# Attention and experts on one core: the experts inside the branch's arms, and the second half's rows in places of their own, read a block ahead

## The chip, the core and the metric

The kernel runs on one core of a Trainium2 chip. Five engines work side by side, each on its own stream of instructions: TensorE (PE) multiplies matrices into PSUM and takes weights in a parallel stream (PEld), VectorE (DVE) and ScalarE (ACT) work elementwise and read PSUM, GpSimd (POOL) makes masks, small sums and the indirect gathers, and SyncE (SP) issues most DMAs. Engines wait for each other by semaphores. The metric is device time in microseconds (us) of one execution; lower is better.

## The reference, cut to what matters

```python
x = L0_attn_x                                     # 2048 tokens x 512
x = layernorm(x + attention(x))                   # 16 heads of 32, causal, q and k of unit norm, rope on every second head
x = layernorm(x + experts(x))

def experts(x):
    scores = softmax(x @ gate_w)                  # 8 experts
    w, e = top_k(scores, 2)
    routed = sum over the two of  w * ((silu(x @ w_gate[e]) * (x @ w_up[e])) @ w_down[e])    # hidden 352
    shared = (silu(x @ sw_gate) * (x @ sw_up)) @ sw_down                                      # hidden 704
    return routed + shared
```

All of it is float32, and layernorm has no weights.

## The kernel before

**A branch, and what follows it.** The kernel loads x and the weights, looks whether all gains of q are small enough for a softmax with a bound fixed in advance, and reads that comparison (`choice`, L1510) into a register of every engine. `tc.If(bounded > 0)` (L1514) then runs `fast_attention`; the other arm (`general_attention`) is not run with these inputs, but lies in the program. Behind the join, `sparse_moe` is called once for both arms (L1537).

**Attention.** `fast_attention` is one long list of steps whose order on PE is written out by hand: x is transposed (L112), multiplied to q, k and v (L126, the rows `fps_qkv`), normed and rotated, and then scores (L331), exponentials (ACT, L341) and values (L376) run in units of heads and 512 keys. At its end come the output product, the first layer norm, the transposes of the result (x1T) and the gate logits (L286). The result goes to DRAM in rows (`x1d`) and, for the second half, transposed (`x1Td`). Into PE's free places of that end the kernel puts six "fillers" (`first_block`, L1452): the six up products of the shared expert's block 0. The shared expert's weights are loaded (`load_shared_expert`, L633) by `x_is_read`, as soon as the space of the transposed x is free.

**The shared expert.** It works in eight blocks b of two tiles (256 tokens). `shared_up_piece` (L664 to L685) makes one of six pieces j of a block's hidden values: a gate product and an up product (8 matmul instructions each, in the rows `ps_gs` and `ps_us`), silu on ACT (L675), the product of the two on DVE (L677; L683 to L685 for the narrow sixth). The PSUM pool for it, `ps_gu`, has two buffers of each kind, so PE's product j + 2 waits until DVE has multiplied piece j. `shared_down` (L964 to L982) multiplies a block's hidden values by the down weights, into one PSUM bank per tile, and hands each to a function `done`.

**First half, routing, experts.** `sparse_moe` (L708) begins with tables (L733 to L766), then makes the softmax of the logits (L796 to L803) and the two largest (L813 to L817) on DVE and ACT, counts the tokens of each expert and gives each a place (L842 to L906). Beside it PE runs blocks 1 to 3 of the shared expert and the down products of blocks 0 to 3. What they give is added to x1 and put away in DRAM (`accd`). Then 36 tiles of 128 routed tokens follow (`routed`, L1116): rows are gathered from `x1d` (L1005), transposed, multiplied by the weights of the tile's expert, whose place PE reads from a table, and written to `yd`. If the routing needs more tiles, a second branch (L1159) runs them; with these inputs it does not.

**Second half.** L1166 to L1185 run blocks 4 to 7 of the shared expert, and with them the end of all 16 tiles: a tile's sum takes two gathered rows of `yd` per token, weighted (`with_experts`, L1041), then the layer norm (L776, of which `inv_sqrt`, L594, is eleven DVE operations on 128x1) and the write to `out` (L1053). In block b the first piece is followed by the last block's down product, by the reads of the block's rows of x1 and of the old sums of the first half (`read_rows`, L1055), and by the read of the next block's x1T (`read_block`). Each later piece is followed by one of four items: two `early_rows` (the gathered rows are added to x1 of this block's tiles) and two `old_rows` (they are added to an old sum, which is then normed and written). Rows and old sums take turns in a pool of five buffers, gathered rows in a pool of four.

**What sets the order.** Where the text says `tc.manual_schedule`, the named engines run the instructions in the order of the program text; the others get an order from a planner. In `sparse_moe` PE and SP are fixed by hand, and DVE, ACT and POOL are planned. Within an engine the order never changes at run time.

## Time and profile before

Three executions took 1158.70, 1160.28 and 1161.79 us: the median is 1160.28. The profile is of another execution.

| quantity | before |
|---|---|
| profiled execution | 1160.72 us |
| its span | 1159.0 us |
| PE busy | 1114.8 us, 96% |
| DVE, ACT, POOL busy | 603.9, 502.3 and 193.0 us |
| mean granted clock of PE | 0.992 of full speed |
| PE's first instruction of the first tile | 5.86 us |
| attention's last product (logits) / first product behind the join | 631.12 / 634.93 us |
| first product of the second half in PE's main flow (block 4, L664) | 1031.19 us |
| last down product's end / last write issued | about 1149.7 / 1155.10 us |

The profile's lines read as follows. A line of the timeline gives the start, the duration, the engine, the line of the program, the operation, the tiles (result<-operands) and their shape; xN means that N equal instructions stand together. In brackets stands how long the engine had been idle before, and what released it: "<-DVE big L677" is DVE's instruction of line 677, "<-issue" means that the profile shows nothing that it waited for. Queues have a q behind their engine's name. The clock column, PEclk, is the share of full speed that the chip granted PE; in a window in which it is 0.50 a matmul takes twice as long.

### The profile page before, as it was taken

The numbers are of one execution on the slowest core, as the hardware profiler recorded it, in microseconds if no ns is written. First come the engines' busy times: TensorE is split into PE (matmuls) and PEld (weight loads), VectorE is DVE, ScalarE is ACT, GpSimd is POOL, SyncE is SP. The second block draws the span as 40 slices with busy tenths as digits, with TensorE's granted clock in tenths as the row PEclk, the third lists the DMA queues.
The fourth block names the chain that finished last, engine by engine and source line by source line (L and its number), as shares of the span: only waits on it lengthen the run. The fifth ranks groups of instructions, "written<-read, shape, count | busy, mean of one in ns | idle before, by whom it ended". The sixth has DMA issues, their size and how long they took to land.

```text
span 1159.0 us, 15359 instructions
## 1 busy us (share of the span) xinstructions
PE 1114.8 (96%) x5692; PEld 584.8 (50%) x5692; DVE 603.9 (52%) x948; ACT 502.3 (43%) x847; POOL 193.0 (17%) x207
## 2 busy tenths in 40 slices
PE   7999999999999999999998999999999999999996
PEld 4543333333343333333355777556656565666664
DVE  1566796777777786797856341111111111115666
ACT  3576777878778777665642100111112111110000
POOL 0321213210321213101020010101011010022331
PEclk9998999999999999999999999999999999999999
DMA  9000000000000110122113595322221221033553
GB/s 302 17 1 1 1 1 1 1 1 1 1 1 1 46 46 10 66 64 73 55 47 130 190 329 174 116 64 72 64 64 64 64 67 61 28 121 100 154 162 127
DMA packets 50227, 83.71 MB, mean 72 GB/s; under 512 B 8032, under 2 KB 22368, under 8 KB 50144
## 3 DMA queue, kind: packets, MB, share of 16 engines
q1 hardware_dynamic: 43904, 64.39, 16.3%
q0 software_dynamic: 5440, 17.83, 5.3%
q8 instruction: 50, 0.82, 0.3%
q10 hardware_dynamic: 800, 0.39, 0.2%
q14 instruction: 33, 0.27, 0.1%
HBM read 59.79 MB, written 22.81 MB: 71 GB/s over the span
## 4 chain that ended last, share of the span: by engine, by line
PE 77%; DVE 8%; issue 7%; ACT 3%; DMA 2%; POOL 2%; SPq 0%; POOLq 0%; DVEq 0%; ACTq 0%
PE fps_qkv L126 12%; PE fps_s L331 9%; PE ps_dr L1031 8%; PE ps_gr L1129 7%; PE ps_ur L1129 7%; PE fps_av L376 7%; PE ps_ds L972 6%; PE ps_us L664 5%; PE ps_gs L664 4%; PE fps_o L229 4%; DVE facc L367 3%; ACT big L341 2%; PE ps_xT L1014 1%; DMA y<-yd,slot_i 1%; PE fps_qkT L204 1%
## 5 line engine op out<-in xcount | busy, mean ns | idle before, releaser
L341 ACT ACTIVATE big<-fps_s,neg_gmax 128x1024 f32<-128x1024 f32 (+3 forms) x320 | 296.7, 983 | 85.8 <-PE fps_s L331 84.4
L367 DVE TENSOR_TENSOR facc<-facc,big 128x2048 f32<-128x2048 f32 (+3 forms) x128 | 250.1, 1954 | 58.3 <-POOL big L352 28.9
L126 PE MATMUL fps_qkv<-big,shared 128*128 128x384 f32 x512 | 183.7, 502 | 1.6 <-ACT facc L403 0.8
L331 PE MATMUL fps_s<-big 32*128 32x512 f32 (+3 forms) x1280 | 174.3, 581 | 0.7 <-ACT big L211 0.7
L376 PE MATMUL fps_av<-big 128*32 128x512 f32 (+3 forms) x1280 | 138.2, 538 | 13.8 <-POOL big L352 11.7
L126 PEld LDWEIGHTS fps_qkv<-big,shared 128*128 128x128 f32 x512 | 93.1, 192 | 85.7 <-issue 17.3
L1016 DVE COPY xT<-ps_xT 128x512 f32<-128x512 f32 x34 | 23.5, 691 | 171.3 <-PE ps_xT L1014 171.3
L352 POOL TENSOR_SCALAR_AFFINE_SELECT big<-big 128x512 f32<-128x512 f32 x64 | 61.7, 965 | 306.1 <-ACT big L341 305.7
L331 PEld LDWEIGHTS fps_s<-big 32*128 32x128 f32 x1280 | 55.7, 184 | 92.8 <-issue 53.6
L1031 PE MATMUL ps_dr<-big,hT 128*128 (+1 forms) x216 | 98.7, 593 | 0.5 <-ACT hT L1024 0.5
L1039 ACT COPY y<-ps_dr 128x512 f32<-128x512 f32 x36 | 21.1, 585 | 166.3 <-PE ps_dr L1031 166.3
L1129 PE MATMUL ps_gr<-big,xT 128*128 x288 | 91.2, 459 | 0.0
L1129 PE MATMUL ps_ur<-big,xT 128*128 x288 | 91.2, 459 | 0.0
L376 PEld LDWEIGHTS fps_av<-big 128*32 128x32 f32 x1280 | 31.5, 109 | 106.2 <-issue 76.8
L675 ACT ACTIVATE acts<-ps_gs 128x256 f32<-128x256 f32 x35 | 13.4, 383 | 155.0 <-PE ps_gs L664 150.8
L664 PE MATMUL ps_us<-big,shared 128*128 128x256 f32 x336 | 78.6, 380 | 1.5 <-DVE big L677 1.5
L1005 POOL DMA_INDIRECT rows<-x1d,rows_of x36 | 34.2, 950 | 260.0 <-PE ps_xT L1014 211.9
L1129 PEld LDWEIGHTS ps_gr<-big,xT 128*128 128x128 f32 x288 | 54.4, 189 | 40.4 <-issue 17.1
L664 PE MATMUL ps_gs<-big,shared 128*128 128x256 f32 x280 | 68.7, 389 | 3.5 <-DVE big L760 3.5
L664 PEld LDWEIGHTS ps_us<-big,shared 128*128 128x128 f32 x336 | 63.7, 190 | 10.9 <-DVE big L677 2.3
L1129 PEld LDWEIGHTS ps_ur<-big,xT 128*128 128x128 f32 x288 | 51.9, 190 | 22.8
L1031 PEld LDWEIGHTS ps_dr<-big,hT 128*128 128x128 f32 (+1 forms) x216 | 41.0, 190 | 42.6 <-issue 34.4
(188 smaller groups left out, 1112.6 us busy)
## 6 DMA issues: line engine op xcount, KB each, us to landing
yd<-y SPq DMA_DIRECT2D x36, 256.0 KB, 2.0
big<-in_L_ffn_w_gate_dram SPq DMA_DIRECT2D x8, 704.0 KB, 10.4
big<-in_L_ffn_w_up_dram SPq DMA_DIRECT2D x8, 704.0 KB, 10.4
big<-in_L_attn_x_dram SPq DMA_DIRECT2D x16, 256.0 KB, 4.4
fres<-in_L_attn_x_dram SPq DMA_DIRECT2D x16, 256.0 KB, 2.8
x1d<-big SPq DMA_DIRECT2D x16, 256.0 KB, 2.0
big<-in_L_ffn_w_down_dram SPq DMA_DIRECT2D x8, 512.0 KB, 7.5
x<-x1d SPq DMA_DIRECT2D x12, 256.0 KB, 2.9
```

The costliest lines, as they stand in the source:

```text
L126: nc.tensor.matmul(ps[0], xT[:, t, c * P : (c + 1) * P], wq_sb[c].rearrange("p (s m) -> p s m", s=3)[:, :, g * P : (g + 1) * P], start=(c ...
L229: nc.tensor.matmul(ps[0], xs[t][:, g * P : (g + 1) * P], wo_sb[:, g, :], start=(g == 0), stop=(g == NC - 1))
L331: nc.tensor.matmul(pss[n][i // 2][:, i % 2, off:], k_at[(g * NB + kb) % KV][r, kl, :], q_at[u % Q][r, off:], start=True, stop=True,)
L341: nc.scalar.activation(pr_at[n % PR][:, 2 * j : 2 * j + 2, off:], pss[n][j][:, :, off:], AF.Exp, bias=neg_gmax)
L352: nc.gpsimd.affine_select(d, d, [[0, 4], [1, P]], ALU.is_ge, 0.0, base=0, channel_multiplier=-1)
L367: nc.vector.tensor_tensor(acc[:, :, off:], first[:, :, off:], pr[:, :, off:], ALU.add)
L376: nc.tensor.matmul(avs[g, b][32 * i : 32 * i + 32, off:], v_at[(g * NB + kb) % KV][:, kl, i * HD : (i + 1) * HD], pr_at[n % PR][:, i, off: ...
L664: nc.tensor.matmul(ps.rearrange("p (t m) -> p t m", t=BT), w[:, c, lo : lo + P], x[:, :, c, :], start=(c == 0), stop=(c == NC - 1),)
L972: nc.tensor.matmul(pd, hid[:, j, tl * P : (tl + 1) * P], wd[:, j, :], start=(j == 0), stop=False)
L1005: nc.gpsimd.indirect_dma_start(r, None, x1d, bass.IndirectOffsetOnAxis(ap=rows_of[:, i : i + 1], axis=0))
L1031: nc.tensor.matmul(pd, hT[:w, c, :], big[:w, bass.ds(at_d + (DOWNS + c * DM), DM)], start=(c == 0), stop=(c == NHC - 1),)
L1129: nc.tensor.matmul(ps, xT[:, c, :], big[:, bass.ds(at_e + (at + c * HE), HE)], start=(c == 0), stop=(c == NC - 1),)
```

## The change

- **The experts inside the arms.** `sparse_moe` is called (as `moe`) at the end of each arm and not behind the join. The program holds it twice, and the arm that runs now ends the program with the jump over the other one. The small pool of `general_attention` is opened in its arm.
- **One piece more in the attention's end.** `first_pieces` makes seven fillers: the sixth of block 0 is followed by piece 0 of block 1, whose hidden values go to `HIDS[1]`, and `sparse_moe` leaves that piece out.
- **Products on the identity.** `keep_busy` runs 16 128x128 products of the identity with itself ahead of the branch, and 6 behind the first tile's transposes. Nothing reads them.
- **Space.** The rope table lies in `shared`, behind x transposed, and the shared expert is loaded eight tile steps later; `ones`, the starts of tiles and a sum lie in `big`.
- **Second half.** PE, SP, DVE, POOL and ACT all run in the order of the text. Gathered rows have eight places, and rows and old sums sixteen more, all in `big` (`place_at`). Ahead of block 4 the old sums, the next block's x1T and the rows are read and the gathers of four tiles are issued; afterwards each item issues the gathers of the item four further on, and a block's rows and old sums are read in the block before. In a block the two old items now come first, in steps 2 and 3, the early ones in steps 4 and 5. The layer norm is split: statistics on DVE, the root and the product with the mean as four small POOL operations (`roots`), and, one step later, the scaling on ACT (`scaled`).
- **The end.** The last block's down product runs tile by tile (`apart=True`), and its layer norm (`last_done`) starts from a root by ACT's Ln and Exp (`inv_sqrt_seed`, L606) with one step of three DVE operations (`inv_sqrt_step`, L616). The table for them is loaded ahead of that product.

```diff
@@ -443,8 +443,9 @@
             for step in queue.pop(0)[1]:
                 step()
             if not read and (not queue or queue[0][0] is None):
+
                 read.append(n)
-                x_is_read()
+                later(8, x_is_read)
...
@@ -488,6 +489,7 @@
 
             banks(0, 2, 3)
             x_transposed(0)[0]()
+            keep_busy(psum("fps_busy"), 6)
...
-HID0 = 5 * GW
+HIDS = 5 * GW, DOWNS + 5 * DW
...
-        def shared_down(b, done):
+        def shared_down(b, done, apart=False):
             hid = hid_of(b)
             pds = [ps_d.tile([P, DM], F32, tag="d", name=f"ps_ds{b * BT + tl}") for tl in range(BT)]
+            def rest(tl):
+                rows = slice(tl * P // 2, (tl + 1) * P // 2)
+                nc.tensor.matmul(
+                    pds[tl], hid[rows, CH - 1, tl * P : (tl + 1) * P], wd[rows, CH - 1, :], start=False, stop=True
+                )
             for tl, pd in enumerate(pds):
                 for j in range(CH - 1):
                     nc.tensor.matmul(
                         pd, hid[:, j, tl * P : (tl + 1) * P], wd[:, j, :], start=(j == 0), stop=False
                     )
-            for tl, pd in enumerate(pds):
-                rows = slice(tl * P // 2, (tl + 1) * P // 2)
-                nc.tensor.matmul(
-                    pd, hid[rows, CH - 1, tl * P : (tl + 1) * P], wd[rows, CH - 1, :], start=False, stop=True
-                )
-            for tl, pd in enumerate(pds):
-                done(b * BT + tl, pd)
+                if apart:
+                    rest(tl)
+                    done(b * BT + tl, pd)
+            if not apart:
+                for tl in range(BT):
+                    rest(tl)
+                for tl, pd in enumerate(pds):
+                    done(b * BT + tl, pd)
...
@@ -1040,24 +1043,57 @@
             nc.sync.dma_start(yd[i * P : (i + 1) * P, :], y)
-        def with_experts(t, acc):
+        brought, gathers = {}, [0]
+        def bring(t):
             for k in range(2):
-                y = m4.tile([P, DM], F32, tag="y", name=f"y{k}_{t}")
+                y = place_at(gathers[0] % (2 * AHEAD))
+                gathers[0] += 1
                 nc.gpsimd.indirect_dma_start(
                     y, None, yd, bass.IndirectOffsetOnAxis(ap=slot_i[:, k, t : t + 1], axis=0)
                 )
+                brought[t, k] = y
+        def with_experts(t, acc):
+            for k in range(2):
+                y = brought.pop((t, k))
                 nc.vector.scalar_tensor_tensor(acc, y, tops[k][:, t : t + 1], acc, ALU.mult, ALU.add)
-        def finish(t, acc):
-            layer_norm(acc, acc, t)
+        norm_at = big[:, 3 * GW : 3 * GW + 5 * NT].rearrange("p (i t) -> p i t", i=5)
+        norms = lambda i, t, n=1: norm_at[:, i, t : t + n]
+        scalings = []
+        def statistics(t, acc):
+            stats = m2.tile([P, 6], F32, tag="ln_stats", name=f"stats{t}")
+            nc.vector.bn_stats(stats, acc)
+            nc.vector.bn_aggr(norm_at[:, 0:2, t], stats)
+        def roots(t, n):
+            nc.gpsimd.tensor_scalar(norms(2, t, n), norms(1, t, n), EPS_LN, None, ALU.add)
+            nc.gpsimd.tensor_tensor(norms(2, t, n), norms(2, t, n), norms(4, t, n), ALU.pow)
+            nc.gpsimd.tensor_tensor(norms(3, t, n), norms(0, t, n), norms(2, t, n), ALU.mult)
+            nc.gpsimd.tensor_scalar(norms(3, t, n), norms(3, t, n), -1.0, None, ALU.mult)
+        def scaled(t, acc):
+            nc.scalar.activation(acc, acc, AF.Identity, bias=norms(3, t), scale=norms(2, t))
             nc.sync.dma_start(out[0, t * P : (t + 1) * P, :], acc)
+        AHEAD = 4
+        place_at = lambda i: big[:, 4 * GW + i * DM : 4 * GW + (i + 1) * DM]
         def read_rows(b):
             for t in range(b * BT, (b + 1) * BT):
-                row_of(t)
+                held[t] = place_at(2 * AHEAD + t - HALF)
+                nc.sync.dma_start(held[t], x1d[t * P : (t + 1) * P, :])
+        def read_old(b):
             for t in range(b * BT - HALF, (b + 1) * BT - HALF):
-                held[t] = m5.tile([P, DM], F32, tag="row", name=f"old{t}")
+                held[t] = place_at(2 * AHEAD + HALF + t)
                 nc.sync.dma_start(held[t], accd[t * P : (t + 1) * P, :])
         def early_rows(t):
@@ -1066,12 +1102,26 @@
         def old_rows(t):
             acc = held.pop(t)
             with_experts(t, acc)
-            finish(t, acc)
+            statistics(t, acc)
+            roots(t, 1)
+            scalings.append((step[0] + 1, lambda: scaled(t, acc)))
         def second_done(t, pd):
             acc = held.pop(t)
             nc.vector.tensor_tensor(acc, pd, acc, ALU.add)
-            finish(t, acc)
+            statistics(t, acc)
+            if t % BT == BT - 1:
+                roots(t - 1, 2)
+            scalings.append((step[0] + 1, lambda: scaled(t, acc)))
+        def last_done(t, pd):
+            acc = held.pop(t)
+            nc.vector.tensor_tensor(acc, pd, acc, ALU.add)
+            statistics(t, acc)
+            seed = inv_sqrt_seed(nc, m2, norms(1, t), EPS_LN, f"ln{t}")
+            inv_sqrt_step(nc, m2, norms(2, t), norms(1, t), EPS_LN, seed, f"ln{t}")
+            nc.vector.tensor_scalar(acc, acc, norms(0, t), norms(2, t), ALU.subtract, ALU.mult)
+            nc.sync.dma_start(out[0, t * P : (t + 1) * P, :], acc)
...
-                    shared_up(b, j)
+                    if (b, j) != (1, 0):
+                        shared_up(b, j)
...
@@ -1163,13 +1214,24 @@
             hT = hidden_transposed(last[0], last[1])
             down(last[0], hT, last[2])
-        with in_order():
+        ET = mybir.EngineType
+        step = [0]
+        with tc.manual_schedule(engines={ET.PE, ET.SP, ET.DVE, ET.Pool, ET.Activation}):
+            nc.gpsimd.memset(norm_at[:, 4, :], -0.5)
             work = {}
             for b in range(NBL // 2, NBL):
                 first = b * BT
-                work[b] = [lambda t=first + k: early_rows(t) for k in range(BT)]
-                work[b] += [lambda t=first - HALF + k: old_rows(t) for k in range(BT)]
+                work[b] = [(old_rows, first - HALF + k) for k in range(BT)]
+                work[b] += [(early_rows, first + k) for k in range(BT)]
+            items = [item for b in range(NBL // 2, NBL) for item in work[b]]
+            read_old(NBL // 2)
+            read_block(NBL // 2 + 1)
+            read_rows(NBL // 2)
+            for _, t in items[0:AHEAD]:
+                bring(t)
+            del items[0:AHEAD]
             for b in range(NBL // 2, NBL):
                 for j in range(CH):
                     if (b, j) != (NBL // 2, 0):
@@ -1177,12 +1239,27 @@
                     if j == 0:
                         if b > NBL // 2:
                             shared_down(b - 1, second_done)
-                        read_rows(b)
-                        if b + 1 < NBL:
+                    while scalings and scalings[0][0] <= step[0]:
+                        scalings.pop(0)[1]()
+                    if j >= 2:
+                        add, t = work[b][j - 2]
+                        add(t)
+                        if items:
+                            bring(items.pop(0)[1])
+                    if b + 1 < NBL:
+                        if j == 1 and b + 1 > NBL // 2 + 1:
                             read_block(b + 1)
-                    elif work[b]:
-                        work[b].pop(0)()
-            shared_down(NBL - 1, second_done)
+                        elif j == 2:
+                            read_old(b + 1)
+                        elif j == 3:
+                            read_rows(b + 1)
+                    step[0] += 1
+            while scalings:
+                scalings.pop(0)[1]()
+            nc.scalar.preload_act_table_set("natural_log_exp_and_others")
+            shared_down(NBL - 1, last_done, apart=True)
...
+    def keep_busy(ps, n):
+        for _ in range(n):
+            nc.tensor.matmul(ps[:, 0:P], ident, ident, start=True, stop=True)
+
+    with tc.tile_pool(name="ps_busy", bufs=1, space=PSUM) as ps_busy:
+        keep_busy(ps_busy.tile([P, P], F32, name="busy"), 16)
...
+        return [piece(0, j) for j in range(CH)] + [piece(1, 0)]
...
         with tc.If(bounded > 0) as branch:
             xT = shared[:, 0 : NT * DM].rearrange("p (t m) -> p t m", t=NT)
-            fast_attention(
-                tc, mem, xT, xa, x, x1d, wq_sb, wo_sb, gain, rope_sb, gw, logits, ident, neg_gmax, asmall, load_shared,
-                x1T_kept, x1T_done, first_block,
-            )
+            with tc.tile_pool(name="fsmall", bufs=3) as fsmall:
+                fast_attention(
+                    tc, mem, xT, xa, x, x1d, wq_sb, wo_sb, gain, rope_sb, gw, logits, ident, neg_gmax, fsmall,
+                    load_shared, x1T_kept, x1T_done, first_pieces, keep_busy,
+                )
+            moe()
         with branch.Else():
-            general_attention(tc, mem, shared, x1d, xs, wq_sb, wo_sb, gain, rope_sb, ident, pow_mh, layer_norm, asmall)
...
+            moe()
-    sparse_moe(tc, big, shared, xs, ident, logits, w_gate, w_up, w_down, x1d, x1Td, x1T_kept, yd, accd, out)
```

## The prediction

> **What bounds the kernel now.** I read the page's busy shares and chain first, then what TensorE (PE) waited for, then the timeline and the clock around each of those waits.
>
> ```profile
> PE 1114.8 (96%) x5692; PEld 584.8 (50%) x5692; DVE 603.9 (52%) x948; ACT 502.3 (43%) x847; POOL 193.0 (17%) x207
> ...
> PE 77%; DVE 8%; issue 7%; ACT 3%; DMA 2%; POOL 2%; SPq 0%; POOLq 0%; DVEq 0%; ACTq 0%
> ```
>
> PE is busy for 1114.8 of 1159.0 us, so what can be won without removing products is at most the 44.2 us in which it stands, and the time in which its clock is low. The list of PE's waits (total, times, longest) gives those that the diff touches:
>
> ```profile
> PE fps_xT L112 <- POOL ones L68: 5.9, 1, 5.9
> PE ps_us L664 <- DVE big L677: 4.2, 3, 2.7
> PE ps_gs L664 <- DVE big L760: 3.5, 1, 3.5
> ...
> PE ps_gs L664 <- ACTq L1159: 1.4, 1, 1.4
> ```
>
> Its largest entry, L376 behind POOL L352 (11.7), lies in the attention's middle, where PE's order stays as it was. Around the join behind the attention's branch the timeline reads (start, duration, instruction, in brackets the idle time before it):
>
> ```profile
> 631.12 0.33 PE L286 MATMUL fps_logits<-ident,fby_e 128*128 128x128 f32 x1 [0.41 <-ACT fby_e L305]
> ...
> 633.60 1.28 ACT L800 ACT_TABLE_LOAD   x1 [2.54 <-issue]
> 634.67 0.23 DVE L760 CAST big<-big 128x128 f32<-128x128 int32 x1 [2.99 <-issue]
> 634.93 3.58 PE L664 MATMUL ps_gs<-big,shared 128*128 128x256 f32 x8 [3.48 <-DVE big L760]
> ...
> 638.35 1.89 PE L664 MATMUL ps_us<-big,shared 128*128 128x256 f32 x8
> ```
>
> ACT and DVE wait for nothing but the jump ("issue"), PE for DVE behind it. The same eight matmuls then take 3.58 us and next time 1.89. The table of 1 us windows (PE, PEld, DVE, ACT, POOL, PEclk, DMA, GB/s) says why: the granted clock is 0.50.
>
> ```profile
> 636.00:637.00 1.00, 1.00 (x4) 0.82 (x3) 0.80 (x3) 0.10 (x1) 0.00 (x0) 0.50 0.01 4
> ...
> 1049.00:1050.00 1.00, 1.00 (x4) 0.82 (x3) 0.98 (x3) 0.00 (x0) 0.69 (x2) 0.50 0.47 184
> ```
>
> The second row is the shared expert's second half, whose first gather starts at 1033.70:
>
> ```profile
> 1033.70 0.94 POOL L1046 DMA_INDIRECT y<-yd,slot_i  x1 [62.72 <-DMA x<-x1d]
> ...
> 1039.64 2.20 DVE L1049 SCALAR_TENSOR_TENSOR x<-y,top,x 128x512 f32<-128x512 f32 x3 [4.20 <-DMA y<-yd,slot_i]
> ...
> 1047.49 0.41 DVE L677 TENSOR_TENSOR big<-ps_us,acts 128x256 f32<-128x256 f32 x1
> ...
> 1047.95 3.59 PE L664 MATMUL ps_us<-spare,shared 128*128 128x256 f32 x8 [2.68 <-DVE big L677]
> ```
>
> DVE stands in front of additions whose rows have not come, the multiplication L677 queues behind them, and PE gets no free PSUM bank. Start and end:
>
> ```profile
> 5.86 1.09 PE L112 MATMUL fps_xT<-ident,big 128*128 128x128 f32 x4 [5.86 <-POOL ones L68]
> ...
> 7.68 5.49 PE L126 MATMUL fps_qkv<-big,shared 128*128 128x384 f32 x8 [0.74 <-ACT shared L113]
> ...
> 1148.57 1.13 PE L978 MATMUL ps_ds<-shared,big 64*128 64x512 f32 x4
> 1149.73 0.69 DVE L1073 TENSOR_TENSOR x<-ps_ds,x 128x512 f32<-128x512 f32 x1 [0.67 <-PE ps_ds L978]
> ...
> 1155.10 0.98 SPq L1053 DMA_DIRECT2D out_dram<-x  x2
> 1155.18 0.55 DVE L783 TENSOR_SCALAR x<-x,mv,rstd 128x512 f32<-128x512 f32 x1
> ```
>
> **The sum's base.** All rows come from the execution of 1160.72 us (span 1159.0 and 1.72 around it), 0.44 above the median of 1160.28. Between 640 and 1020 PE is busy without a gap (the window 640 to 680 has 40.00 of 40), so a saving before it arrives whole behind it. About 0.3%, 3.5 us, is what a measurement tells from no change.
>
> **Start.** Added: 16 matmuls on the identity ahead of the branch, 6 behind the first transposes. One is two instructions of 128 columns; a pair of that shape (L833, L834) starts every 0.11 us at full clock, 0.21 at half by the same count. The identity is ready at 1.5 and the first starts near 1.7: 32 instructions end at 8.5 if all run at half clock, at 6.8 if the clock rises after 3.4 us. I take the middle, 7.65, instead of 5.86: 1.8 lost. The first transposes then take 0.5 instead of 1.09, the six fill 1.28, over the 0.74 gap in which ACT copies, and the eight qkv products run from about 9.4 at 2.8 us instead of 5.49. They ended at 13.0 and would end at 12.2, and the twelve transposes behind them, still partly slow now, give 0.2 more. Gain 1.0. Bounds: -2 (the matmuls only delay, the clock rises no sooner) to +2 (they end before the branch).
>
> **Join.** The experts now follow in the branch's arm: no jump. Piece (1,0) (16 matmuls) moves ahead of it onto the attention's banks, in the same place of PE's order. Recoverable are the 3.48 idle and 3.58 - 1.89 = 1.69 of low clock: 5.17. What is late next: PE runs the piece from 631.45 to 634.9, and the shared down product waits for its multiplication on DVE to free banks. That stands behind the logits' copy (631.7), maximum and subtraction (632.5), ACT's table load and exponential (1.28 and 0.31) and the sums, then a second table load and silu (0.38) and 0.42 for itself: about 635.6 if the first load is done ahead. So 0.7 stall, gain 4.5 (bounds 0, the wait reappears whole, to 5.2). Where the hand-over costs nothing else, the cover is these 3.4 us of products.
>
> Changed at no price: the blank writes and the delayed reading of the shared expert. The latter ran at 476 and is first used at 589; eight tiles later still leaves tens of us.
>
> **Second half.** Removed: the 2.68 wait, 3.59 - 1.89 = 1.70 of low clock, and two waits for L677 at 1082.85 and 1112.68 (0.75 and 0.73): 5.9. The wait of 1.36 at L1159 stays. Added: on SP, one block's rows are read ahead (same DMAs, other time); on POOL, eight gathers stand at the front and four tiny operations per layer norm (rows of 128x1: 0.1 to 0.13) replace eleven on DVE of 0.15, which DVE has to spare (13.88 busy of 40 in 1020 to 1060); ACT gets 128x512 scalings (0.63 by L404). By the pitch of 1.25 and landings of 2.3 to 6.0 us in the old trace the second gather is there near 1041, the fourth near 1043.5. The fixed order asks for them in steps 2 and 3 of block 4: the multiplication behind them must run by about 1043.1 and 1046.6 for PE not to wait. That leaves 2 and 3 us. Silu now queues on ACT behind a scaling, that behind POOL's powers, these behind gathers: up to 5.8 us may pass there before PE notices. The next block's x, read 5.9 us behind the down product, has 9.6 us of room for a landing of 5.6. Gain 5.9 if nothing is late; bounds 6.5 and -12 (next part).
>
> One row decides 1.70 of it: after 2.68 us of idling the clock was 0.50 for 3.4 us. The Trainium skill (TensorE: Matmul & The Clock Gate, "Why this matters for your kernels") allows gaps up to about 3 us without a drop; by it the second half would give 4.2, the sum 11.3, and 1149.4. The trace disagrees, so the row counts.
>
> **End.** The last down product is finished tile by tile and the last layer norm takes ACT's Ln and Exp (0.2 each) and three DVE operations instead of eleven interleaved for two tiles. Now 1149.73 to 1155.73. Then: addition 1150.45, statistics and aggregate 1151.4, seed 1151.9, steps and scaling 1153.0: 2.7 earlier. But the jump over the other arm, long as it now is, comes at the end: 2.5 to 3.0 of "issue" as at the join, behind SP's last issue near 1153.4, then 0.4 and 0.9 of semaphores and drains as now: 1157.4 instead of 1159.0. Gain 1.6 (0.9 to 2.7). The Trainium skill (Runtime: NRT & Kernel Launch, "Instruction fetch mechanics") has a taken branch out of the loaded window wait for its target; without that the end would give 2.7, the sum 14.1.
>
> **Sum.** 1.0 + 4.5 + 5.9 + 1.6 = 13.0; 1160.72 - 13.0 = 1147.7, 1147.3 against the median. I say 1147.5.
>
> **The rivals.**
> - *The join's wait only moves.* DVE's softmax chain and two table loads (2.6) still lie before the piece's multiplication; if PE idles 3.5 there and the clock drops, the join gives 0: 1160.72 - 8.5 = 1152.2. For it: silu is ready only at 639.89 now. Against: its time runs from 631.5 then. Chance 0.17.
> - *Gathers still late in block 4.* Landings up to 6.0 are in the trace; 2.68 + 1.70 stay, the second half gives 1.5: 1152.1. Chance 0.15.
> - *The matmuls at the start only delay.* Start -2.0: 1150.7. Chance 0.10.
> - *Other side: the order by hand holds DVE.* Before, DVE's order was planned; now a multiplication stands fixed behind additions that wait for gathers, in all four blocks. If each block pays what block 4 pays now (2.68 + 1.70 = 4.4), 17.5 are lost for 5.9: 1147.7 + 17.5 = 1165.2. It decides from 13.0, 3.25 per block; slower by 0.3% from 4.1. For it: POOL's slot waits of 2.27 now come from such coupling. Against: after the front, each gather has a whole block. Chance 0.08.
> - *It doesn't do what it says.* The jump costs at the end what it cost at the join and all gaps move: join 0, end 0, second half 1.5: about 1158.2. Chance 0.06.
>
> **How the numbers follow.** My forecast holds 0.44; its own range is 1145 to 1149.5. The moderate rivals (0.42) give 1150.7 to 1152.2, two together up to 1156.5, 1158.2 holds 0.06 and 1165.2 holds 0.08. So 8 in 10 lie in 1143.5 to 1156. Faster (below 1156.8) 0.85, within 0.3% 0.07, slower (above 1163.8) 0.08.
>
> **What the changed profile would show.** Right: PE's waits without L760; no clock of 0.50 near 635 and 1049; qkv's first eight near 2.8 us; the first down product of the experts near 4.5 us sooner; out's last issue near 1143 and "issue" of 2.5 or more behind it. Wrong: PE standing behind L677 in each of blocks 4 to 7, ACT's silu waiting for POOL, or PE waiting at the first ps_ds for 3 us.

## The result and the profile after

The changed kernel took 1147.62 us (median of four, 1147.21 to 1149.25) against 1159.88 before: the ratio is 0.9893, with a 95% interval of 0.9878 to 0.9909. The profiled execution took 1147.72 with a span of 1146.0, so between the two profiled executions 13.0 us are gone; the medians differ by 12.3. One execution among all the runs below, of the old second half, took 3032.82 us at full clock; nothing recorded shows why, and no number below contains it.

The list of what TensorE (PE) waited for, in the changed kernel (total, times, longest; lines have moved, L664 is now L667 and L677 is L680):

```profile
PE fps_av L376 <- POOL big L352: 11.7, 14, 2.7
...
PE busy L1489 <- POOL ident masks.py:199: 1.6, 1, 1.6
...
PE ps_gs L667 <- ACTq L1210: 0.7, 1, 0.7
...
PE ps_ds L975 <- DVE big L680: 0.6, 1, 0.6
```

The wait of 5.9 at the start is one of 1.6, the 3.5 at the join is one of 0.6 at the first down product, and the 4.2 behind DVE's multiplication in the second half is gone. The attention's 11.7 is as it was.

PE's timeline at the places that the prediction named (start, duration, instruction, idle before it in brackets):

```profile
1.58 6.37 PE L1489 MATMUL busy<-ident 128*128 128x128 f32 x32 [1.58 <-POOL ident masks.py:199]
7.79 0.60 PE L112 MATMUL fps_xT<-ident,big 128*128 128x128 f32 x4
8.23 1.50 PE L1489 MATMUL fps_busy<-ident 128*128 128x128 f32 x12
9.57 2.75 PE L126 MATMUL fps_qkv<-big,shared 128*128 128x384 f32 x8
12.15 1.47 PE L112 MATMUL fps_xT<-ident,big 128*128 128x128 f32 x12
13.46 2.82 PE L126 MATMUL fps_qkv<-big,shared 128*128 128x384 f32 x8
...
629.60 0.33 PE L286 MATMUL fps_logits<-ident,fby_e 128*128 128x128 f32 x1 [0.41 <-ACT fby_e L305]
629.76 1.89 PE L667 MATMUL ps_gs<-big,shared 128*128 128x256 f32 x8
631.49 1.89 PE L667 MATMUL ps_us<-big,shared 128*128 128x256 f32 x8
633.97 8.85 PE L975 MATMUL ps_ds<-shared,big 128*128 128x512 f32 x20 [0.59 <-DVE big L680]
...
1024.55 1.99 PE L667 MATMUL ps_gs<-spare,shared 128*128 128x256 f32 x8 [0.72 <-ACTq L1210]
```

The first eight qkv products take 2.75 and not 5.49. Behind the logits PE goes on at once, at full clock, and waits 0.59 ahead of the first down product. The end reads:

```profile
1126.69 4.46 PE L975 MATMUL ps_ds<-shared,big 128*128 128x512 f32 x10
1131.08 1.12 PE L969 MATMUL ps_ds<-shared,big 64*128 64x512 f32 x2
1132.13 4.56 PE L975 MATMUL ps_ds<-shared,big 128*128 128x512 f32 x10
1136.62 1.12 PE L969 MATMUL ps_ds<-shared,big 64*128 64x512 f32 x2
...
1140.51 0.55 DVE L1123 TENSOR_SCALAR big<-big 128x512 f32<-128x512 f32 x1
1141.08 0.33 SPq L1124 DMA_DIRECT2D out_dram<-big  x1
```

Between marks that both profiles have, the 13.0 us divide like this (before, after, difference):

| stretch | before | after | gained | predicted |
|---|---|---|---|---|
| start, to the second group of qkv | 14.57 | 13.46 | 1.1 | 1.0 |
| from there to the logits | 616.55 | 616.14 | 0.4 | 0 |
| logits to the experts' first down product | 8.95 | 4.37 | 4.6 | 4.5 |
| from there to the second half's main flow | 391.12 | 390.58 | 0.5 | 0 |
| second half, to the last down product | 108.71 | 102.14 | 6.6 | 5.9 |
| last down product | 9.80 | 11.05 | -1.25 | 0 |
| from its end to the end of the span | 9.30 | 8.26 | 1.0 | 1.6 |

The marks say where the time went, not which edit did it. That is what the runs were for.

### The profile page after: what moved, and what is told of

Its sections match the earlier page's. It is cut to its first block, busy times and chain, and to the rows that moved or that the text cites. A ratio compares the mean times of both kernels' runs of the same rounds, so it can differ in the third digit from the quotient of the medians.

```text
span 1146.0 us, 15267 instructions
## 1 busy us (share of the span) xinstructions
PE 1114.8 (97%) x5736; PEld 588.2 (51%) x5736; DVE 583.9 (51%) x764; ACT 514.6 (45%) x866; POOL 209.2 (18%) x252
## 5 line engine op out<-in xcount | busy, mean ns | idle before, releaser
L126 PE MATMUL fps_qkv<-big,shared 128*128 128x384 f32 x512 | 181.0, 497 | 0.9 <-ACT facc L403 0.8
L376 PE MATMUL fps_av<-big 128*32 128x512 f32 (+3 forms) x1280 | 137.8, 537 | 13.7 <-POOL big L352 11.7
L352 POOL TENSOR_SCALAR_AFFINE_SELECT big<-big 128x512 f32<-128x512 f32 x64 | 61.8, 966 | 305.6 <-ACT big L341 305.2
L667 PE MATMUL ps_us<-big,shared 128*128 128x256 f32 x336 | 78.4, 379 | 0.0
L1180 PEld LDWEIGHTS ps_gr<-big,xT 128*128 128x128 f32 x288 | 54.4, 189 | 40.4 <-issue 17.1
L667 PEld LDWEIGHTS ps_us<-big,shared 128*128 128x128 f32 x336 | 63.8, 190 | 8.6
L667 PE MATMUL ps_gs<-big,shared 128*128 128x256 f32 x280 | 67.0, 382 | 0.0
```

Source lines behind the costliest of these rows:

```text
L126: nc.tensor.matmul(ps[0], xT[:, t, c * P : (c + 1) * P], wq_sb[c].rearrange("p (s m) -> p s m", s=3)[:, :, g * P : (g + 1) * P], start=(c ...
L352: nc.gpsimd.affine_select(d, d, [[0, 4], [1, P]], ALU.is_ge, 0.0, base=0, channel_multiplier=-1)
L376: nc.tensor.matmul(avs[g, b][32 * i : 32 * i + 32, off:], v_at[(g * NB + kb) % KV][:, kl, i * HD : (i + 1) * HD], pr_at[n % PR][:, i, off: ...
L667: nc.tensor.matmul(ps.rearrange("p (t m) -> p t m", t=BT), w[:, c, lo : lo + P], x[:, :, c, :], start=(c == 0), stop=(c == NC - 1),)
L1180: nc.tensor.matmul(ps, xT[:, c, :], big[:, bass.ds(at_e + (at + c * HE), HE)], start=(c == 0), stop=(c == NC - 1),)
```

## The experiments

All are the changed kernel with one edit, unless said otherwise, and are set against its 1147.62. Comments behind # in the diffs are this text's; some stand for code that is left out. The kernel before was run again beside each group of runs, and its median lay between 1158.46 and 1159.88; so a difference of about 1 us between two medians shows little by itself, and the marks in the traces have to bear it.

### The join

**The experts behind the join again.**

```diff
                     load_shared, x1T_kept, x1T_done, first_pieces, keep_busy,
                 )
-            moe()
         with branch.Else():
...
                     piece()
-            moe()
+        moe()
```

> The changed kernel with the experts behind the join again, once for both arms; the seventh filler stays ahead of it. Theory (the jump itself stops TensorE): TensorE idles about 3.5 us at the join and then runs at half clock, 5.2 in place of the 0.6 that it now waits, while the end loses its jump (1.7): 1147.6 + 4.6 - 1.7 = 1150.5. Rival (the piece moved ahead of the join is what covers it): TensorE waits under 1.5 us there, its clock stays, and without a jump at the end the time is 1146 to 1147.

Measured: 1146.76 us (1145.96 to 1149.18), ratio to before 0.9891 (0.9868 to 0.9913). The timeline of this run, PE's part and then DVE's:

```profile
629.25 0.33 PE L286 MATMUL fps_logits<-ident,fby_e 128*128 128x128 f32 x1 [0.41 <-ACT fby_e L305]
629.41 1.89 PE L667 MATMUL ps_gs<-big,shared 128*128 128x256 f32 x8
631.14 1.89 PE L667 MATMUL ps_us<-big,shared 128*128 128x256 f32 x8
633.62 8.85 PE L975 MATMUL ps_ds<-shared,big 128*128 128x512 f32 x20 [0.59 <-DVE big L680]
```

```profile
633.14 0.42 DVE L680 TENSOR_TENSOR big<-ps_us,big 128x256 f32<-128x256 f32 x1 [3.33 <-PE ps_us L667]
636.46 0.18 DVE L759 CAST big<-table 128x39 f32<-128x39 int32 x1 [2.90 <-issue]
```

DVE pays 2.90 for the jump as ever, and PE does not notice: 4.37 from the logits to the down product, exactly as without a jump. PE's own jump is hidden too. The list of the branch's instructions (L1604; shortest/median/longest in ns, first and last start) shows that PE's sequencer took it at 629.4, while the queued products ran; it is recorded with 3.76 us there:

```profile
L1604 PEldq COMPARE_BRANCH  x2: 93/1928/3762, 5.6 to 629.4; - x2
```

The expected 3.5 of idling is not there, so the first theory is refuted and the rival holds. The end, without a jump behind it, takes 6.6 us from the last product (1137.72) to the end of the span (1144.3) instead of 8.3. The median shows 0.9 of these 1.7.

**Six fillers.** Piece (1,0) is computed by the experts' own code; the experts stay in the arms.

```diff
-        return [piece(0, j) for j in range(CH)] + [piece(1, 0)]
+        return [piece(0, j) for j in range(CH)]
...
-                    if (b, j) != (1, 0):
-                        shared_up(b, j)
+                    shared_up(b, j)
```

> The changed kernel with piece (1,0) computed by the experts' own code, not as a seventh filler; TensorE's order is the same, only the PSUM banks differ. Theory (the jump was what cost): the first down product starts within 0.7 us of 633.97, the time is 1147.6 to 1148.3. Rival (the hand-over of the attention's banks costs TensorE what the jump cost): a wait of 2 to 3.5 us ahead of that piece, then half clock for some, 1150 to 1153.

Measured: 1147.28 us (1147.07 to 1148.73). From the logits (630.97) to the first down product (635.14) are 4.17 us, with a wait of 0.3 for DVE ahead of the piece and none behind it. So the hand-over of the banks costs nothing, and **either** edit closes the join: no jump, or a piece of work ahead of it. The two do not add up.

### The second half

**The old second half in the changed kernel.** Pools, reads, planned order and layer norm of lines 1041 to 1185 of the kernel before.

```diff
-        with tc.manual_schedule(engines={ET.PE, ET.SP, ET.DVE, ET.Pool, ET.Activation}):
+        with in_order():                    # PE and SP alone
...
-            shared_down(NBL - 1, last_done, apart=True)
+            shared_down(NBL - 1, second_done)
```

> The changed kernel with the second half as it was (pools of five rows and four gathered rows, reads in the same block, order of DVE, ACT and POOL planned, old layer norm to the end); start, join and arms stay changed. Theory (second half and end each give what their marks show): from the first product of the main flow to the last product's end 118.5 us instead of 113.2, and behind it 11 instead of 8.3, since the old end now has the far jump behind it: 1147.6 + 8 = 1155.6. Rival (the gain there came with the shift of the parts ahead): under 1151.

Measured: 1157.28 us (seven executions, 1155.31 to 1160.10; ratio to before 0.9974, 0.9954 to 0.9994), 1.7 above the theory. From the main flow's first product (1025.71) to the last product's end (1146.66) 120.95 us, against 113.19, with waits behind L680 of 5.4 in three, and 11.1 behind it instead of 8.3. In the kernel before the same stretch took 118.5. Here the clock fell for two windows (a loss of 3.4 us), there for one (1.7), and one of the waits is 3.65 instead of 2.68. So the second half is worth at least the 5.3 that the marks give it together with the last product, and the old end with the far jump behind it costs 2.9 more.

**Only PE and SP by hand; DVE, POOL and ACT planned.** Places and early reads as in the changed kernel.

```diff
-        with tc.manual_schedule(engines={ET.PE, ET.SP, ET.DVE, ET.Pool, ET.Activation}):
+        with tc.manual_schedule(engines={ET.PE, ET.SP}):
```

> The changed kernel with only TensorE and SP in the order of the text in the second half, as before; DVE, POOL and ACT are planned, rows are read ahead as in the changed kernel. Theory (early reads are what pays): within 1 us of 1147.6 and TensorE without a wait over 1 us behind L680. Rival (the order by hand pays): waits of 2 to 3 us behind L680 return in one block or more, 1150 to 1154.

Measured: 1160.17 us (ten executions, 1157.64 to 1165.42): the ratio to the kernel before is 1.0002 (0.9985 to 1.0019). One line of the program takes the whole gain. The profiled execution is 14.5 us longer than that of the changed kernel: 10.3 from the main flow's first product to the last down product, 1.6 behind the last product, and 2.6 ahead of the second half, which the edit does not touch. PE's timeline in this run, then DVE's, then one read of SP's:

```profile
1042.99 1.99 PE L667 MATMUL ps_us<-spare,shared 128*128 128x256 f32 x8 [1.65 <-DVE big L680]
...
1049.19 2.98 PE L667 MATMUL ps_us<-big,shared 128*128 128x256 f32 x8 [2.48 <-DVE big L680]
...
1077.80 1.99 PE L667 MATMUL ps_us<-big,shared 128*128 128x256 f32 x8 [1.27 <-DVE big L680]
...
1108.70 1.99 PE L667 MATMUL ps_us<-big,shared 128*128 128x256 f32 x8 [1.61 <-DVE big L680]
```

```profile
1039.31 2.71 DVE L1061 SCALAR_TENSOR_TENSOR big<-big,top 128x512 f32<-128x512 f32 x4
1041.93 0.69 DVE L1071 BATCH_NORM_STATS2 stats<-big 128x6 f32<-128x512 f32 x1
1042.53 0.41 DVE L680 TENSOR_TENSOR big<-ps_us,acts 128x256 f32<-128x256 f32 x1
...
1047.39 1.41 DVE L1061 SCALAR_TENSOR_TENSOR big<-big,top 128x512 f32<-128x512 f32 x2 [1.95 <-DMA big<-yd,slot_i]
1048.72 0.42 DVE L680 TENSOR_TENSOR big<-ps_us,acts 128x256 f32<-128x256 f32 x1
...
1075.88 1.54 DVE L1061 SCALAR_TENSOR_TENSOR big<-big,top 128x512 f32<-128x512 f32 x2 [3.86 <-DMA big<-accd]
1077.33 0.42 DVE L680 TENSOR_TENSOR big<-ps_us,acts 128x256 f32<-128x256 f32 x1
```

```profile
1070.79 0.93 SPq L1097 DMA_DIRECT2D big<-accd  x2
```

The planner puts four additions and statistics ahead of one multiplication, and two additions whose row has not come ahead of the next. The first gather is issued as early as in the changed kernel, 2.75 us behind the main flow's first product in both. But the planner moves the additions forward with the reads: by 1057.5, before block 5 begins at 1062.45, DVE has made sixteen of them, those of blocks 4 and 5, and at 1075.88, in block 5, it stands before the additions of block 6, whose old sums SP has read only at 1070.79. (The same happens a block later, at 1106.77.) Of the 7.0 us that PE waits, 1.65 are thus behind additions that DVE could do later, and 5.4 behind additions that themselves wait for an operand, asked for a block too early. Reading ahead alone therefore does not remove the waits. The run plans ACT and POOL too (the first scaling waits 9.10 us for POOL instead of 5.60), and what each engine's order is worth by itself was not tried. In the changed kernel the same stretch has a multiplication between any two items:

```profile
1035.59 0.75 DVE L1061 SCALAR_TENSOR_TENSOR big<-big,top 128x512 f32<-128x512 f32 x1 [0.20 <-issue]
1036.37 0.69 DVE L1071 BATCH_NORM_STATS2 stats<-big 128x6 f32<-128x512 f32 x1
1037.10 0.18 DVE L1072 BATCH_NORM_AGGREGATE big<-stats 128x2 f32<-128x6 f32 x1
1037.20 0.40 DVE L680 TENSOR_TENSOR big<-ps_us,acts 128x256 f32<-128x256 f32 x1
1037.52 1.53 DVE L1061 SCALAR_TENSOR_TENSOR big<-big,top 128x512 f32<-128x512 f32 x2
```

**One item ahead instead of four.** The order by hand stays. With AHEAD the places for gathered rows go from eight to two as well.

```diff
-        AHEAD = 4
+        AHEAD = 1
```

> The changed kernel with AHEAD = 1: the order by hand stays, but an item's two gathers are issued only behind the addition of the item before. An item then takes some 6.7 us (gathers, landing, additions) where TensorE gives it 3.45. Theory of the rival with the other sign (DVE fixed behind late gathers holds TensorE): TensorE stands behind the multiplication L680 by 3 us in each block, with the clock halved after some, 1158 to 1166. Against it (the slack of the order absorbs it): no wait over 1 us there, under 1150.

Measured: 1174.36 us (two executions, 1172.85 and 1175.87), 1.3% slower than the kernel before and 8 above the expected range. PE's waits:

```profile
PE ps_us L667 <- DVE big L680: 10.5, 3, 5.5
PE ps_ds L969 <- DVE big L687: 6.6, 1, 6.6
```

One wait in each of the four blocks: 5.48, 2.34, 2.68 and 6.64, so 17.1 in all, and the second half with the last down product takes 138.3 us instead of 113.2. In the windows of 1 us the clock loses 8.5 in that stretch; the two make 25.6, where the stretch is 25.1 longer. This is the mechanism of the rival with the other sign, in a kernel made to have it, and it is dearer than the 17.5 that the rival was given. The order pays only where the rows are there when it asks for them: in these runs each of the two, order and early reads, is worth nothing or less without the other.

### The end

**The last down product not tile by tile.**

```diff
-            shared_down(NBL - 1, last_done, apart=True)
+            shared_down(NBL - 1, last_done)
```

> The changed kernel with the last down product not tile by tile (both tiles' 64-row products adjacent again, as in the other blocks); the new last layer norm stays. In the profile the adjacent four take 1.1 us, one tile's two alone 1.05 each, so TensorE ends 1.2 us sooner; DVE then has both tiles' additions, statistics and scalings behind it, 2.0 to 2.6 more. Theory: 0.8 to 1.4 longer, 1148.4 to 1149.0. Rival (the order tile by tile gives nothing): 1146.8 to 1147.6.

Measured: 1150.51 us (1149.28 to 1151.38). By marks, from the last down product's start (1128.40) to the span's end (1149.6), 21.2 us against 19.3 (1126.69 to 1146.0): 1.9 longer. PE is 1.25 faster, and DVE, in its fixed order, finishes the first tile, its wait for ACT included, before it adds the second. The median is 2.9 longer, twice the most that the theory had. The other 1 us would be the clock's: this run's profiled execution lost 5.1 us to it in the attention, the changed kernel's 1.7, but that is seen in one execution each.

**The 64-row products between the tiles.**

```diff
+            if apart:
+                most(0, True, False)      # the first tile's 128-row products
+                rest(0, False, True)
+                rest(1, True, False)      # both tiles' 64-row products, adjacent
+                done(b * BT, pds[0])
+                most(1, False, True)
+                done(b * BT + 1, pds[1])
```

> The changed kernel with one change in the last down product: the 64-row products of both tiles stand together between the first tile's 128-row products and the second's, so that they run side by side again and the first tile is still done early. Theory (the 64-row products of the two tiles overlap only when adjacent, 1.1 us for all instead of 2.1): 1.0 to 1.2 less, 1146.5. Rival (the overlap is no matter of their order): 1147.6.

Measured: 1146.20 us (1145.90 to 1147.29). PE's timeline:

```profile
1126.34 4.45 PE L974 MATMUL ps_ds<-shared,big 128*128 128x512 f32 x10
1130.73 1.13 PE L968 MATMUL ps_ds<-shared,big 64*128 64x512 f32 x4
1131.79 4.56 PE L974 MATMUL ps_ds<-shared,big 128*128 128x512 f32 x10
```

The four stand in 1.13 where two alone took 1.12, and the product with what follows takes 18.3 us instead of 19.3. That much of the gain is shown. The medians differ by 1.4, but the kernel before took 1158.46 beside this run and 1159.88 beside the changed kernel, and by the ratios (0.9889 and 0.9893) only 0.5 is left.

**The arms exchanged**, so that the far jump comes at the start.

```diff
-        nc.vector.tensor_scalar(small_gain, neg_gmax, -GAIN_MAX, None, ALU.is_ge)
+        nc.vector.tensor_scalar(small_gain, neg_gmax, -GAIN_MAX, None, ALU.is_lt)
...
         with tc.If(bounded > 0) as branch:
-            # fast_attention and moe
+            # general_attention and moe
         with branch.Else():
-            # general_attention and moe
+            # fast_attention and moe
```

> The changed kernel with the branch's arms exchanged (the comparison is turned round), so that the arm that runs comes last in the program: the far jump is made at the start, and none at the end. Theory (the jump is 2.8 us after SP's last issue, of which 1.7 are not covered by the landing of the output; at the start it runs beside the products on the identity, which last until 7.8): 1.7 less, 1145.9. Rival (TensorE's own jump at the start costs as much as it saved at the end): the first transposes start near 10.5 instead of 7.79, and the time is 1147.6 to 1148.7.

Measured: 1153.46 us (1153.06 to 1154.46), 5.8 more. At the end the jump is gone: 6.5 us behind the last product instead of 8.3, as expected. At the start it costs far more than at the end:

```profile
1.59 6.03 PE L1489 MATMUL busy<-ident 128*128 128x128 f32 x32 [1.59 <-POOL ident masks.py:199]
11.45 1.09 PE L112 MATMUL fps_xT<-ident,big 128*128 128x128 f32 x4 [3.83 <-issue]
12.33 2.77 PE L1489 MATMUL fps_busy<-ident 128*128 128x128 f32 x12
14.89 3.52 PE L126 MATMUL fps_qkv<-big,shared 128*128 128x384 f32 x8
```

```profile
L1604 PEldq COMPARE_BRANCH  x1: 5921/5921/5921, 5.4 to 5.4; - x1
```

PE's branch lasts from 5.4 to 11.3, the clock falls in the meantime, and the second group of qkv starts at 19.55 instead of 13.46. POOL goes on only at 11.73. Neither theory had that: both took the 2.8 of SP at the end. PE's own taken branch is recorded with 3.54 us at the join of the kernel before and with 3.38 at the end of the changed kernel, there under queued products; here it is 5.9, and the queued products end at 7.62. The trace shows what comes later. A packet of the instruction queue q8 starts 0.9 to 1.4 us behind PE's taken branch at the old join, at the changed kernel's end and in the run with the experts behind the join, and 3.4 to 3.6 us behind it here; it takes about 1 us each time. In the windows 4 to 8 and 8 to 12 us the DMA engines are fully busy with x and the weights (367 and 320 GB/s). That the fetch of the far instructions waits for them fits; no run took that load away, so the load as the cause is not shown.

### The start, and both good edits together

**Without the products on the identity.**

```diff
-    with tc.tile_pool(name="ps_busy", bufs=1, space=PSUM) as ps_busy:
-        keep_busy(ps_busy.tile([P, P], F32, name="busy"), 16)
...
-            keep_busy(psum("fps_busy"), 6)
```

> The changed kernel without the 16 and the 6 products on the identity. Theory (they raise the clock before the first qkv products): those eight take about 5.5 us again instead of 2.75, the second group of qkv starts near 14.5 instead of 13.46, and the whole is 1.1 us longer, 1148.7 against 1147.6. Rival (they only delay the start): the second group starts no later than 13.5 and the time is 1147.6 or less.

Measured: 1146.38 us (1146.26 to 1148.31), and not 1148.7. The second group of qkv starts at 13.09. By its letter the rival came out. But the profiled execution is the only one of all profiles in which the clock did not fall at all in the attention. The windows of 1 us (PE, PEld, DVE, ACT, POOL, PEclk, DMA, GB/s) of this run:

```profile
89.00:90.00 1.00, 1.00 (x12) 0.42 (x4) 0.90 (x2) 0.36 (x1) 0.86 (x1) 1.00 0.00 0
```

and of the changed kernel, both behind PE's wait of 2.65 us for POOL's mask (L352):

```profile
89.00:90.00 1.00, 1.00 (x8) 0.23 (x6) 0.90 (x2) 0.00 (x0) 1.00 (x1) 0.50 0.06 16
```

So this pair cannot tell the products' worth, which is the reason for the next two runs.

**Join back and 64-row products between, with and without the products on the identity.**

> The changed kernel with the experts behind the join again (once for both arms) and the 64-row products between the two tiles' others: the two edits that were faster alone (0.9 and 1.4 less). Theory (independent; the seventh filler covers the join, and no jump is left at the end): 1145.3. Rival (the one gain hides the other): 1146.2 to 1146.8.

> The same without the products on the identity. In the profiles the second group of qkv starts at 12.35 to 13.79 with them and at 13.09 and 14.57 without: theory (they are worth 1.0 on average): 1146.3, 1.0 above its neighbour with them. Rival (without them the clock falls less often later on, as in the run without them, which was 1.2 faster): 1144.1, and a clock loss near 87 us of 0 in the profile instead of 1.7.

Measured: 1145.31 us (1145.14 to 1147.06; ratio to before 0.9885, 0.9870 to 0.9900) with them, 1145.14 (1144.36 to 1149.08; 0.9885, 0.9869 to 0.9900) without. The time is the expected one, 2.3 below the changed kernel, but by the ratios to the kernel before (0.9885 and 0.9893) only 0.9, inside both intervals. The trace shows the sum better: from the last down product's start (1126.88) to the span's end (1143.4) are 16.5 us instead of 19.3, which is both gains whole. Without the products neither theory came out: the time lies between the two, and the clock's loss is not 0. The five executions without the products fall into 1149.06 and 1149.08 on one side and 1144.36 to 1145.14 on the other. The profiled one is of 1149.06; its second group of qkv starts at 14.61, and it lost 5.1 us to the clock in the attention, where its neighbour (1145.14, start at 13.72) lost 1.7: 0.9 and 3.4 make 4.3, where the two differ by 3.9. Over the profiles, the second group starts at 12.93 on average with the products (nine, 12.35 to 13.79) and at 14.09 without (three, 13.09 to 14.61): the 1.2 at that mark are there, but in the median of the whole the runs do not show them.

**Exchanged arms with the 64-row products between.**

> Arms exchanged and 64-row products between the tiles, both together: 1.7 + 1.1 less, 1144.8, if the two are independent; 1145.9 or 1146.5 if one of them gives nothing.

Measured: 1152.60 us (1151.58 to 1153.49) and not 1144.8, 0.9 below the exchanged arms alone. It repeats both findings: PE's branch lasts 5.98 us at the start, and the four 64-row products stand in 1.13.

## Why the prediction was right, and where not

The time (1147.5 forecast, 1147.62 measured) and most terms came out; two of the reasons did not. That the sum of 13.0 came out to the tenth is luck: the end gave 1.8 less than forecast, and the second half gave 0.7 and stretches that were put at nothing 0.9 more.

- **Start, 1.0: right in size at its mark (1.1).** The identity's products ended at 7.95 (7.65 forecast) and qkv took 2.75. Over the profiles the mark is 1.2 earlier with the products, so they do more than delay there. That it arrives whole at the end is not shown; of the two runs with both good edits the one without the products is even 0.2 faster.
- **Join, 4.5: the size right (4.6), the cause half right.** "No jump" was taken as what frees the 5.17, and the piece as cover for DVE's softmax chain behind it. With the jump back, PE waits the same 0.59; with the piece back, 0.3: either alone is enough. The piece covers the jump because PE's branch is taken while its products are still queued, and because DVE's multiplication is done before DVE jumps. The wait forecast as 0.7 behind the softmax chain was 0.59, but by luck: with the jump back it is 0.59 too, where the chain comes only later and DVE has stood idle for 3.33 us before its multiplication. The way from the last up product over DVE to the next product is enough to explain it. The rival "the join's wait only moves" did not happen.
- **Second half, 5.9: 6.6 up to the last down product, the reason incomplete.** The waits went, as listed. They were put down to late gathers, and so to reading ahead; the run with a planned order reads as early and still waits 7.0. That DVE stands in front of additions whose rows have not come describes 5.4 of these 7.0 too. What failed is the step from there to the cure: rows read earlier are only asked for earlier as long as the planner sets DVE's order, and the fixed order, which the prediction names only as a danger, is the other half of the gain. Of its signs of being wrong, ACT's silu behind POOL did appear (the first scaling waits 5.60 us for POOL, silu behind it), but PE loses nothing by it. The rival "gathers still late in block 4" did not happen: DVE waits 2.37 us for the first row, at 1034.63, and PE not at all.
- **End, 1.6: it gave nothing, -0.2 (the last two rows of the table).** The layer norm is 2.7 shorter, as reckoned (3.3 us from the addition to the last scaling, 6.0 before). The jump is as reckoned too: SP branches at 1141.5 and its next instruction is at 1144.3, then 1.6 of semaphores and drains instead of 1.3. Left out was the price of tile by tile on PE: "the last down product is finished tile by tile" was costed at nothing, and it costs 1.25, since two tiles' 64-row products run side by side only when adjacent.
- **Nothing for the rest: 0.9.** 0.5 ahead of the second half, mostly the wait at the second branch (1.36 before, 0.72 now). 0.4 in the attention is luck: the profiled execution before lost 3.4 us to the clock near 88 us and the one after 1.7. Of these 1.7, 0.7 went into a longer wait for DVE at 522.79 (L271: 0.83 us, 0.15 before); the other 0.6 was not followed up.
- **The rival of the other sign** names a mechanism that exists, as the run with one item ahead shows; with four ahead the rows are there, and it does not set in. What it missed is that the planned order holds DVE in the same way once the reads are early.

The Trainium skill's limit (TensorE: Matmul & The Clock Gate, "Why this matters for your kernels") of about 3 us without a drop is not borne out: the clock fell behind gaps of 2.65 and of 1.77 us (last section). That a taken branch whose target is not loaded waits for its fetch (the Trainium skill, Runtime: NRT & Kernel Launch, "Instruction fetch mechanics") agrees with 2.8 us at the end, 2.90 on DVE at the join and 5.9 on PE at the start.

## What to carry to other kernels

Work that is already queued on the bounding engine hid a jump of all engines here; it was enough to move a piece of the next part ahead of it, and doubling the program in both arms then only added a far jump where nothing covers it. Where an engine serves a bounding one and also does work of its own, look at what the planner puts between two of its services: here early reads gave nothing until that order was fixed, and the fixed order lost more than it gained where its operands were not early. Before a product is split to finish a part early, look whether its narrow pieces run side by side, and keep those adjacent.

## What the hardware showed that was not expected

- **The same gap costs another amount in each execution.** Behind the same wait of 2.65 us near 86 to 89 us (some 6 us later with exchanged arms) the loss of clock (1 - PEclk, summed over windows of 1 us) was 0, 1.7 or 3.4 us, none, one or two stretches of 3.4 us at 0.50. Six of the fourteen profiles:

| run | loss near 88 us | loss near 547 us |
|---|---|---|
| before | 3.4 | 0 |
| changed | 1.7 | 0 |
| without products on the identity | 0 | 0 |
| six fillers | 1.7 | 1.7 |
| last product together | 3.4 | 1.7 |
| both edits, without products on the identity | 3.4 | 1.7 |

  Of the other eight, the old second half lost 3.4 in the first place and seven lost 1.7, and none lost anything in the second (the run with a planned order lost 1.7 near 525 us, behind a wait of 1.94). Near 547 us PE waits 1.77 us for DVE (L416), and the clock fell behind it in three profiles:

```profile
545.73 1.12 PE L229 MATMUL fps_o<-big 128*128 128x512 f32 x2 [1.77 <-DVE big L416]
```

```profile
547.00:548.00 1.00, 1.00 (x8) 0.22 (x5) 0.97 (x2) 0.00 (x0) 0.00 (x0) 0.50 0.00 0
```

  Both lines are of the run with six fillers, the first from PE's timeline, the second from its windows. In the changed kernel's profile the same wait (1.76) left the clock at 1.00. Both places together cost between 0 and 5.1 us, so a difference of up to 5 us between two profiles of this kernel can be clock alone. Products that fill the gap near 88 us were not tried.
- **Adjacent 64-row products of two different tiles overlap fully:** four instructions in 1.13 us, two alone in 1.12.
- **A taken jump lasts 2.3 to 3 us on ACT and DVE at the join and 2.8 on SP at the end; on PE 3.4 to 4.6 at the join or the end, and 5.9 at the start,** where the DMA engines were full.
